# Causal attention scores from three bfloat16 pieces of queries and keys instead of float32 products

## The chip, the cores and the metric

The kernel runs on one core of a Trainium2 chip. A core has five engines that run side by side and meet through semaphores: TensorE (PE in the profile; its weight loads are the rows PEld), VectorE (DVE), ScalarE (ACT), GpSimd (POOL) and SyncE (SP), which issues transfers. TensorE multiplies a stationary matrix, loaded first, with a moving one, and writes to PSUM, which has eight banks of 512 float32 columns. VectorE and ScalarE read PSUM; GpSimd works on SBUF. The metric is the device time of one execution in microseconds. Three runs of the kernel before took 2534.42, 2536.99 and 2536.26 us, median 2536.26.

## The reference

Two layers, each an attention-like part and a feed-forward part, on one sequence of 2048 rows of 128 numbers: a linear recurrence with a gate, a mixture of 8 experts, causal attention with 16 heads of 8 numbers, and a stack of six blocks with windowed attention of 32 rows and a gated feed-forward. The change touches the causal attention alone. Cut to what matters, it computes

```
qkv = x @ W_qkv + b_qkv
q, k, v = jnp.split(qkv, 3, axis=-1)          # then 16 heads of 8 numbers each
scores = jnp.einsum('bhqd,bhkd->bhqk', q, k) * scaling
scores = jnp.where(mask[None, None, :, :], scores, -jnp.inf)
probs = jax.nn.softmax(scores, axis=-1)
out = jnp.einsum('bhqk,bhkd->bhqd', probs, v)
return out.transpose(0, 2, 1, 3).reshape(b, t, c) @ W_o + b_o
```

## The kernel before

`front` runs the recurrence, and a small planner (`Merge`, which pops jobs by due times that the program gives) interleaves the experts, the projections of keys and values and the first of the attention. `stages123` then runs the attention, and `stage4` the six blocks with an order written out by hand. On each engine the instructions run in the order in which the program records them.

The 16 heads stand in `NGRP` = 4 groups of four. A group's keys and queries lie in SBUF with a head's 8 numbers in 32 partitions of their own, so that the products of four heads use four different quarters of TensorE's rows. The rest of each 32 partitions is zero but for one: partition 8 holds 1 in the keys and, once it is known, minus the row's maximum in the queries, so that the second product gives score minus maximum.

There are 16 blocks, a group of heads by 512 query rows (`blocks`). For each block two generators make units:

- `maxima(b)` first projects the block's queries (`pq`, and ScalarE writes `qT` with bias and scale). Then, for each 128 query rows and each chunk of up to 512 keys, it multiplies with the queries as the stationary side (`sc1`), adds the causal mask on the last chunk by a bfloat16 product, and VectorE reduces the maximum. `finish` transposes the maxima (`ptm`) and adds them to the queries.
- `attend(b)` takes 128 keys by up to 512 query rows, with the keys as the stationary side (`sc2`). ScalarE takes the exponential into `ex`, GpSimd zeroes the masked part of the diagonal tiles (`affine_select`), and `weigh` multiplies with the values into `av` in pieces of up to 256 columns.

`attention` pairs the units. A mixed unit has two halves, each with two heads of a maxima unit and the other two heads of an attend unit: four products, the exponentials, a due piece of `av`, the maxima. `catch_up` issues maxima units alone where the maxima are not far enough ahead, and at the end of a block attend units stand alone. All these products rotate through seven PSUM banks (`psum_s`); `av` has the eighth.

`keys` projects a group's keys for 512 rows and ScalarE writes `kT` with the bias. The buffer of `kT` also holds states of the recurrence before that (`ys`, `yt` through `kf`). `_layouts` prepares the weights' arrangement and the bias columns on the host.

Of the kernel before, what the change touches and what calls it, by code (L numbers as in the profile page):

```python
# [93 lines left out]
class Kernel:  # L94
# [102 lines left out]
    def load3(self, w):  # L197
        nc, a = self.nc, self.a
        wqk = w.tile([P, 2, NGRP, P], F32, name="wqk")
        nc.sync.dma_start(wqk, a["wqk1"])  # L200
        bqk = w.tile([P, 2, NGRP], F32, name="bqk")
        nc.sync.dma_start(bqk, a["bqk1"])
        wv = w.tile([P, P], F32, name="wv1")
        nc.sync.dma_start(wv, a["L1_attn_W_qkv"][:, 2 * P : 3 * P])
        wo = w.tile([P, P], F32, name="wo1")
        nc.sync.dma_start(wo, a["L1_attn_W_o"])
        bo = w.tile([P, 1], F32, name="bo1")
        nc.sync.dma_start(bo, a["bo1"])
        self.w3 = wqk, bqk, wv, wo, bo
# [243 lines left out]
    def keys_values(self, pool, psum, x, g, hT3, kT, va):  # L453
        wqk, bqk, wv, wo, bo = self.w3
        hg = hT3[:, g * GW : (g + 1) * GW]
        yield from self.norm_transposed(pool, psum, x, g, hg)
        pv = psum.tile([P, G, P], F32, name="pv", tag="b")
        self.add_row(pv, 1)
        for j in range(G):
            self.pe.matmul(  # L460
                pv[:, j, :], lhsT=hg[:, j * P : (j + 1) * P], rhs=wv, start=False, stop=j == G - 1
            )
        self.dve.tensor_copy(
            va[:, g * G : (g + 1) * G, :, 0:HD1], pv.rearrange("p j (h d) -> p j h d", d=HD1)
        )
        yield 1.3
        yield from self.keys(psum, g, hT3, kT, [0])

    def keys(self, psum, g, hT3, kT, grps):
        wqk, bqk, wv, wo, bo = self.w3  # L470
        hg = hT3[:, g * GW : (g + 1) * GW]
        for grp in grps:
            pk = psum.tile([P, GW], F32, name="pk", tag="b")
            self.pe.matmul(pk, lhsT=wqk[:, 1, grp, :], rhs=hg, start=True, stop=True)
            self.act.activation(
                kT[:, grp, g * GW : (g + 1) * GW], pk, AF.Identity, bias=bqk[:, 1, grp : grp + 1]
            )
            yield 0.9

    def front(self, ctx, merge, psum, kvpool, x, hT3, kT, va, xsT):  # L480


        nc, tc, gps = self.nc, self.tc, self.gps
        bqk = self.w3[1]
        pool_ = ctx.enter_context(tc.tile_pool(name="s1", bufs=2))
# [18 lines left out]
        half = CL * 2 * NCH  # L504
        kf = kT.rearrange("p n t -> p (n t)")
        ys = kf[:, 0:half].rearrange("p (l c k) -> p l c k", c=2, k=NCH)
# [5 lines left out]
        for g in range(NG):  # L512
# [7 lines left out]
        gps.tensor_scalar_mul(w4[:, 2, :], w4[:, 2, :], vec[:, 3:4])  # L520
        gps.tensor_scalar_mul(bqk[:, 0, :], bqk[:, 0, :], HD1 ** -0.5)
        gps.iota(
            self.iota, pattern=[[1, P]], base=-1024, channel_multiplier=0, allow_small_or_imprecise_dtypes=True
# [7 lines left out]
        self.ssm_carry(pool, pw, rows, zy, u)  # L531

        begin = [(0, 9, 43, 51), (10, 22, 58, 66), (7, 41, 74, 87), (16, 57, 91, 111)]
        def ones():
# [6 lines left out]
        for g, (a, b, c, d) in enumerate(begin):  # L541
            wait.append(merge.add(a, self.ssm_out(pool, psum, x, g, gate, own[g], u)))
            wait.append(merge.add(b, self.experts(pool, psum, x, g)))
            merge.add(c, self.keys_values(kvpool, psum, x, g, hT3, kT, va))
            merge.add(d, self.keys(psum, g, hT3, kT, range(1, NGRP)))
        return wait

    def stages123(self, x, xT):
        nc, tc, a = self.nc, self.tc, self.a
        scale = HD1 ** -0.5  # L550
        with ExitStack() as ctx:
# [13 lines left out]
            hT = keep.tile([P, T], F32, name="hT3")  # L565
            kT = keep.tile([P, NGRP, T], F32, name="kT3")
            va = keep.tile([P, NT, HEADS1, 32], F32, name="va")
# [3 lines left out]
            early.__enter__()  # L571
            wait = self.front(early, merge, banks, kvpool, x, hT, kT, va, xsT)

# [10 lines left out]
            def bank(name):  # L584
                return banks.tile([P, GW], F32, name)
# [4 lines left out]
            ends = [sum(size[: i + 1]) for i in range(len(size))]  # L590
            qs, late = {}, []

# [8 lines left out]


            def maxima(b):
                grp, qc = blocks[b]
                if b % NG == 0:
                    qs[grp] = pool.tile([P, T], F32, name="qT3", tag="qT3")
                q = qs[grp]
                cols = slice(qc * GW, (qc + 1) * GW)
                pq = bank("pq")
                pe.matmul(pq, lhsT=wqk[:, 0, grp, :], rhs=hT[:, cols], start=True, stop=True)  # L610
                act.activation(q[:, cols], pq, AF.Identity, bias=bqk[:, 0, grp : grp + 1], scale=scale)
                nm = nms[b % 2]
                for j in range(G):
                    qt = G * qc + j
# [4 lines left out]
                    def part(pr, ch, qt=qt, mx=mx, chunks=chunks, j=j):  # L619
                        c, wd = chunks[ch]  # L620
                        n = len(chunks)
                        scs = []
                        for h in (2 * pr, 2 * pr + 1):
                            r = slice(32 * h, 32 * h + 32)
                            sc = bank("sc1")
                            pe.matmul(
                                sc[:, :wd], lhsT=q[r, qt * P : (qt + 1) * P], rhs=kT[r, grp, c : c + wd],
                                start=True, stop=ch < n - 1,
                            )
                            scs.append((h, sc))  # L630

                        def rest():
# [4 lines left out]
                            if pr and ch == n - 1:  # L637
                                dve.tensor_reduce(
                                    nm[:, j, :].rearrange("p (h s) -> p h s", s=32)[:, :, HD1],
                                    mx[:, :, 0:n], axis=AX.X, op=ALU.max, negate=True,  # L640
                                )

                        return rest

                    for ch, (_, wd) in enumerate(chunks):
                        yield wd, part, ch

                def finish():
                    pt = bank("ptm")
                    for j in range(G):  # L650
                        pe.transpose(pt[:, j * P : (j + 1) * P], nm[:, j, :], self.ident)
                    dve.tensor_tensor(q[:, cols], q[:, cols], pt, ALU.add)

                yield 0, finish, None


# [3 lines left out]
            def attend(b):  # L660
# [15 lines left out]
                for kt in range(last + 1):  # L676
# [3 lines left out]
                    def part(pr, kt=kt, lo=lo):  # L680
                        nonlocal ex
                        if ex is None:
                            ex = pp.tile([P, 4, GW], F32, name="ex3")
                        for jj in range(2):
                            h = 2 * pr + jj
                            r = slice(32 * h, 32 * h + 32)
                            sc = bank("sc2")
                            pe.matmul(
                                sc[:, lo:], lhsT=kT[r, grp, kt * P : (kt + 1) * P],
                                rhs=q[r, qc * GW + lo : (qc + 1) * GW], start=True, stop=True,  # L690
                            )
                            act.activation(ex[:, h, lo:], sc[:, lo:], AF.Exp)

# [132 lines left out]
            def catch_up(b, c):  # L826
                nonlocal ahead
                while ahead is not None and done - ahead[1] < wanted(b, c) - GW:
                    for rest in [step_m(ahead, pr) for pr in range(2)]:
                        rest()  # L830
# [8 lines left out]
            def attention():  # L839
                nonlocal ahead, halves  # L840
                b_now, c_now = -1, 0
                for b, wd, part, whole in ats:
# [5 lines left out]
                    if ahead is not None and done - ahead[1] < wanted(b, c_now):  # L848
                        for half in range(2):
                            rest = step_m(ahead, half)  # L850
                            part(1 - half)
                            weigh_due()
# [6 lines left out]
                    else:  # L859
                        for half in range(2):  # L860
                            part(1 - half)
                        weigh_due()
# [542 lines left out]
def _layouts(x):  # L1405
# [16 lines left out]
    wqk = np.zeros((P, 2, NGRP, 4, 32), f)  # L1422
    wqk[..., :HD1] = x["L1_attn_W_qkv"][:, : 2 * P].reshape(P, 2, NGRP, 4, HD1)
    got["wqk1"] = wqk.reshape(P, 2, NGRP, P)
    bqk = np.zeros((2, NGRP, 4, 32), f)
    bqk[..., :HD1] = x["L1_attn_b_qkv"][: 2 * P].reshape(2, NGRP, 4, HD1)
    bqk[1, ..., HD1] = 1.0
    got["bqk1"] = bqk.reshape(2, NGRP, P).transpose(2, 0, 1)
    got["bv1"] = x["L1_attn_b_qkv"][2 * P :].reshape(1, P)
# [30 lines left out]
```

## Time and profile before

| | before |
|---|---|
| median of three runs | 2536.26 us |
| the profiled execution's own time | 2534.71 us |
| its span | 2533.0 us |
| mean granted TensorE clock | 0.975 |
| TensorE busy | 2423.0 us (96%) |
| VectorE busy | 1844.1 us (73%) |
| ScalarE busy | 1728.4 us (68%) |
| GpSimd busy | 1471.4 us (58%) |

The profiler records start and end of each instruction of one execution. A row of a group names engine and operation, the tiles written and read (`sc<-kT,qT`), the shapes and the count. Since every instruction passes through one helper, all have line L66, and one goes by tiles. A matmul's end is modelled, so the distance from one start to the next says more than its length. In the trace both kinds of products write a tile `sc`: `sc<-kT,qT` with keys moving is that of the maxima, `sc<-qT,kT` that of the exponentials. In a window's row, the columns are the length, busy time and instructions of PE, PEld, DVE, ACT and POOL, the granted clock, the share of the DMA engines and GB/s.

### The profile page before, as it was taken

The page shows a single profiled execution, that of the slowest core. Times are in us where ns is not written, and L with a number is a line of the kernel's source. Part 1 is how long each engine was busy: PE and PEld are TensorE (multiplying, and loading weights), DVE is VectorE, ACT ScalarE, POOL GpSimd, SP SyncE. Part 2 cuts the span into 40 slices and gives each one's busy share as a digit, 9 for nine tenths or more (in the row PEclk, how much of TensorE's full clock was granted, in tenths as well). Part 3 has the DMA queues.
Part 4 walks back from the last instruction along what each step waited for, and adds up shares of the span by engine and source line. Part 5 has one row for each costly group of instructions (what it writes and reads, how often), then busy time and mean ns, then how long its engine had stood idle before and what let it go on. Part 6 is the DMA issues. An engine that isn't in the chain of part 4 may idle for free.

```text
span 2533.0 us, 87720 instructions
## 1 busy us (share of the span) xinstructions
PE 2423.0 (96%) x38312; PEld 1441.2 (57%) x38312; DVE 1844.1 (73%) x2519; ACT 1728.4 (68%) x3233; POOL 1471.4 (58%) x1007
## 2 busy tenths in 40 slices
PE   5689999999999799999999999999999999999997
PEld 3663333333334466666666666666666666666665
DVE  7667765467653488887888778877888778878874
ACT  3323455634556377887888878887888788888884
POOL 3210000100001699888888878887888888888880
PEclk8889999989999899999999999999999999999999
DMA  2000000000000422233223322242223322222221
GB/s 79 1 1 1 1 1 1 1 1 2 1 1 1 103 70 71 68 90 77 70 70 78 93 62 70 66 101 66 72 67 91 76 70 70 67 60 64 65 68 38
DMA packets 100157, 130.13 MB, mean 51 GB/s; under 512 B 26553, under 2 KB 47681, under 8 KB 99777
## 3 DMA queue, kind: packets, MB, share of 16 engines
q1 hardware_dynamic: 99196, 124.07, 19.8%
q8 instruction: 304, 4.98, 0.9%
q14 instruction: 77, 0.62, 0.1%
q10 hardware_dynamic: 580, 0.46, 0.1%
HBM read 23.50 MB, written 1.05 MB: 10 GB/s over the span
## 4 chain that ended last, share of the span: by engine, by line
PE 90%; DVE 4%; ACT 3%; POOL 1%; issue 1%; DMA 0%; ACTq 0%; DVEq 0%; POOLq 0%
PE sc L66 21%; PE ps L66 14%; PE po L66 9%; PE pt L66 7%; PE pv L66 7%; PE px L66 7%; PE av L66 6%; PE ph L66 5%; PE py L66 4%; PE ptp L66 3%; PE prb L66 1%; PE pvar L66 1%; PE pm L66 1%; ACT ex L66 1%; DVE kT L66 1%
## 5 line engine op out<-in xcount | busy, mean ns | idle before, releaser
L66 POOL TENSOR_TENSOR rn<-ss,mhalf 128x32 f32<-128x32 f32 x96 | 524.2, 5460 | 8.0
L66 ACT ACTIVATE sm<-sm,mx,rn 128x64 f32<-128x64 f32 x1536 | 519.8, 429 | 3.7 <-POOL mx L66 3.0
L66 DVE TENSOR_REDUCE mx<-sc 128x1 f32<-128x512 f32 (+3 forms) x640 | 353.5, 604 | 222.3 <-PE sc L66 220.9
L66 ACT ACTIVATE ex<-sc 128x512 f32<-128x512 f32 (+3 forms) x640 | 306.1, 537 | 281.5 <-PE sc L66 280.4
L66 POOL TENSOR_TENSOR rot_a<-rot_a,rot_b 128x1024 f32<-128x1024 f32 x192 | 449.9, 2361 | 5.7 <-DVE rot_b L66 5.7
L66 PE MATMUL sc<-kT,qT 64*32 64x64 f32 (+2 forms) x13568 | 442.0, 259 | 8.6 <-ACT qT L66 7.8
L66 PE MATMUL ps<-wqkv,s 128*128 128x512 f32 x768 | 395.3, 619 | 2.0 <-DVE s L66 1.6
L66 POOL TENSOR_SCALAR_AFFINE_SELECT ex<-ex 128x512 f32<-128x512 f32 x64 | 40.6, 635 | 576.0 <-ACT ex L66 560.2
L66 PE MATMUL sc<-qT,kT 32*128 32x512 f32 (+3 forms) x1280 | 339.1, 581 | 4.0 <-DVE qT L66 2.1
L66 DVE TENSOR_TENSOR rot_a<-ps,tab 128x1024 f32<-128x1024 f32 x192 | 234.8, 1223 | 127.1 <-ACT sq L66 122.0
L66 PEld LDWEIGHTS sc<-kT,qT 64*32 64x32 f32 (+1 forms) x13568 | 219.5, 113 | 188.6 <-issue 108.7
L66 PEld LDWEIGHTS po<-pT,vw 64*64 64x64 f32 x12288 | 210.5, 135 | 184.9 <-issue 175.6
L66 ACT ACTIVATE sq<-ps 128x1024 f32<-128x1024 f32 x192 | 196.5, 1023 | 134.3 <-PE ps L66 97.1
L66 PE MATMUL po<-pT,vw 64*64 64x32 f32 x12288 | 242.1, 222 | 4.6 <-ACT pT L66 4.2
L66 DVE TENSOR_TENSOR rot_b<-ps,tab 128x1024 f32<-128x1024 f32 x192 | 232.9, 1213 | 0.0
L66 DVE TENSOR_REDUCE ss<-sq 128x16 f32<-128x1024 f32 x192 | 224.6, 1211 | 1.1
L66 PE MATMUL pt<-ident,rot_a 128*128 128x128 f32 x1536 | 211.4, 281 | 11.6 <-POOL rot_a L66 11.5
L66 PEld LDWEIGHTS pt<-ident,rot_a 128*128 128x128 f32 x1536 | 170.8, 142 | 46.4 <-issue 23.7
L66 PE MATMUL pv<-wqkv,s 128*128 128x512 f32 x384 | 190.6, 619 | 0.0
L66 PE MATMUL px<-oT,wo 64*128 64x128 f32 x3072 | 185.8, 276 | 0.8 <-DVE ot L66 0.8
L66 POOL TENSOR_TENSOR rot_a<-rot_a,rn 128x1024 f32<-128x1024 f32 x96 | 182.6, 1902 | 0.1
L66 PEld LDWEIGHTS px<-oT,wo 64*128 64x128 f32 x3072 | 176.6, 189 | 9.0 <-issue 4.5
(212 smaller groups left out, 3481.8 us busy)
## 6 DMA issues: line engine op xcount, KB each, us to landing
vw<-vt SPq DMA_DIRECT2D x1524, 64.0 KB, 2.0
wqkv<-in_L_ffn_Wqkv SPq DMA_DIRECT2D x18, 512.0 KB, 5.5
wo<-in_L_ffn_Wo SPq DMA_DIRECT2D x24, 256.0 KB, 6.0
w<-in_L_ffn_W SPq DMA_DIRECT2D x6, 341.0 KB, 3.6
x<-in_L_attn_hidden_states SPq DMA_DIRECT2D x4, 256.0 KB
out<-ot SPq DMA_DIRECT2D x4, 256.0 KB, 2.3
rot<-in_rot SPq DMA_DIRECT2D x1, 960.0 KB
w<-in_L_ffn_W SPq DMA_DIRECT2D x12, 64.0 KB, 4.9
```

Of the source, the lines that this page charges most:

```text
L66: return self._tc.keep_in_program_order(call(*args, **kw))
```

## The change

Queries and keys are no longer float32 but three bfloat16 pieces: the value rounded, the remainder rounded, and the remainder of that. A head's 32 partitions hold the three pieces of a key in partitions 0 to 23 (8 each), and ones in 24 to 26. The queries have three copies, `q[:, 0]`, `q[:, 1]` and `q[:, 2]`, and copy i repeats piece i in partitions 0 to 7, 8 to 15 and 16 to 23. A product of copy i with the keys so adds piece i times all three key pieces, and three products accumulated in PSUM make all nine pairs. The maximum, too, is split in three pieces, in partitions 24 to 26 of copy 0.

- `keys` has, after ScalarE's instruction, one of VectorE that forms the remainder (`krest`) and two of GpSimd that form the second piece and write `kT`. The bias table `bqk` has two more rows: the bias where ScalarE writes, and zeros and ones that choose partitions.
- `project` replaces the projection in `maxima`: ScalarE writes copy 0, VectorE the remainder (`qrest`), GpSimd copies 1 and 2. It is called for the next block after the first unit of a block (for the first block at its start), and the scale is folded into `wqk`.
- A unit's `part` returns its products as functions, and `products` issues them in turn: the first product of all heads, then the second, then the third. In a mixed half that is two heads of either kind, elsewhere four heads of one kind. Each product is now a weight load and a matmul of their own.
- The maxima of a block collect in `m`, and `pieces_of` splits them with six GpSimd instructions into `nm`.
- `kT` and the queries of head groups 0 and 2 share the buffer that `kf` had; those of groups 1 and 3 have one of their own.

```diff
     def keys(self, split, psum, g, hT3, kT, grps):
...
+            one, two = (split.tile([P, GW], BF16, name=f"k{i}") for i in range(2))
+            rest = split.tile([P, GW], F32, name="krest")
             self.act.activation(
-                kT[:, grp, g * GW : (g + 1) * GW], pk, AF.Identity, bias=bqk[:, 1, grp : grp + 1]
+                one, pk, AF.Identity, bias=bqk[:, 2, grp : grp + 1], scale=bqk[:, 3, 0:1]
             )
+            self.dve.scalar_tensor_tensor(rest, pk, bqk[:, 1, grp : grp + 1], one, ALU.add, ALU.subtract)
+            self.gps.tensor_scalar_mul(two, rest, bqk[:, 3, 1:2])
+            self.gps.tensor_tensor(kT[:, grp, g * GW : (g + 1) * GW], rest, two, ALU.subtract)
...
+        gps.tensor_scalar_mul(wqk[:, 0], wqk[:, 0], HD1 ** -0.5)
...
+            def project(b):
+                grp, qc = blocks[b]
+                q, cols = qs[grp], slice(qc * GW, (qc + 1) * GW)
+                pq = bank("pq")
+                pe.matmul(pq, lhsT=wqk[:, 0, grp, :], rhs=hT[:, cols], start=True, stop=True)
+                rest = pool.tile([P, GW], F32, name="qrest")
+                act.activation(q[:, 0, cols], pq, AF.Identity, bias=bqk[:, 0, grp : grp + 1])
+                dve.scalar_tensor_tensor(
+                    rest, pq, bqk[:, 0, grp : grp + 1], q[:, 0, cols], ALU.add, ALU.subtract
+                )
+                gps.tensor_copy(q[:, 1, cols], rest)
+                gps.tensor_tensor(q[:, 2, cols], rest, q[:, 1, cols], ALU.subtract)
+
+            def products(heads):
+                for i in range(3):
+                    for product in heads:
+                        product(i)
...
-                            pe.matmul(
-                                sc[:, :wd], lhsT=q[r, qt * P : (qt + 1) * P], rhs=kT[r, grp, c : c + wd],
-                                start=True, stop=ch < n - 1,
-                            )
+                            def product(i, r=slice(32 * h, 32 * h + 32), sc=sc):
+                                pe.matmul(
+                                    sc[:, :wd], lhsT=q[r, i, qt * P : (qt + 1) * P], rhs=kT[r, grp, c : c + wd],
+                                    start=i == 0, stop=i == 2 and ch < n - 1,
+                                )
...
                     for ch, (_, wd) in enumerate(chunks):
                         yield wd, part, ch
+                        if j == 0 and ch == 0 and b + 1 < len(blocks):
+                            project(b + 1)
...
+            def pieces_of(m, nm):
+                out = nm.rearrange("p j (h s) -> p j h s", s=32)
+                for i in range(2):
+                    piece = pool.tile([P, G, 4], BF16, name="m_piece")
+                    gps.tensor_copy(piece, m)
+                    gps.tensor_copy(out[:, :, :, 3 * HD1 + i], piece)
+                    left = m if i == 0 else out[:, :, :, 3 * HD1 + 2]
+                    gps.tensor_tensor(left, m, piece, ALU.subtract)
...
                         for half in range(2):
-                            rest = step_m(ahead, half)
-                            part(1 - half)
+                            m_heads, rest = step_m(ahead, half)
+                            heads, exps = part(1 - half)
+                            products(m_heads + heads)
+                            exps()
                             weigh_due()
```

## The prediction

> **What bounds the kernel now.** I read the page first: the TensorE row of part 2 and the chain in part 4.
>
> ```profile
> PE 2423.0 (96%) x38312; PEld 1441.2 (57%) x38312; DVE 1844.1 (73%) x2519; ACT 1728.4 (68%) x3233; POOL 1471.4 (58%) x1007
> ...
> PE   5689999999999799999999999999999999999997
> ...
> PE 90%; DVE 4%; ACT 3%; POOL 1%; issue 1%; DMA 0%; ACTq 0%; DVEq 0%; POOLq 0%
> ```
>
> TensorE sets the time nearly everywhere. The change lies in the causal attention, from the first `sc` group at 183 us to about 823 us, so next I cut the span there.
>
> ```profile
> 0.00:183.00 183.00, 127.09 (x761) 98.27 (x761) 131.10 (x369) 58.00 (x150) 47.88 (x123) 0.88 0.09 28
> 183.00:823.00 640.00, 623.44 (x5407) 241.28 (x5407) 378.32 (x748) 329.92 (x681) 42.95 (x66) 0.97 0.01 1
> ```
>
> The columns after the length are busy PE, PEld, DVE, ACT and POOL, then granted clock. In the attention PE is busy 97%, VectorE 59%, GpSimd 7%. Shorter products therefore show, until VectorE's maxima limit. Third, one stretch in order of time (start, length):
>
> ```profile
> 269.37 1.56 PE L66 MATMUL sc<-kT,qT 32*128 32x512 f32 x10
> ...
> 270.53 4.87 DVE L66 TENSOR_REDUCE mx<-sc 128x1 f32<-128x512 f32 x8 [0.41 <-PE sc L66]
> 270.76 0.59 PE L66 MATMUL sc<-kT,qT 32*128 32x512 f32 x2
> ...
> 275.29 0.70 PE L66 MATMUL sc<-kT,qT 32*128 32x512 f32 x2
> ...
> 275.30 0.70 PE L66 MATMUL sc<-qT,kT 32*128 32x512 f32 x2
> ...
> 275.82 0.59 PE L66 MATMUL sc<-kT,qT 32*128 32x512 f32 x2
> 275.83 0.59 PE L66 MATMUL sc<-qT,kT 32*128 32x512 f32 x2
> ```
>
> A float32 product is two records (passes). Four heads start within 20 ns, at 275.29, and their second passes start together 0.53 later; the first of these contains about 0.10 of weight load. At 269.37 ten records fill 1.56: two groups of four and two more, with passes 0.43 apart once rolling: 269.91, 270.34 and, in the line shown, 270.76. Eight maxima back to back take 4.87, 0.60 each. Fourth, what a full-array pass and bfloat16 cost:
>
> ```profile
> 1132.09 1.88 PE L66 MATMUL ps<-wqkv,s 128*128 128x512 f32 x4
> ```
>
> ```profile
> 116.41 0.40 PE L66 MATMUL pi<-ident,which 128*128 128x128 bf16 x4 [1.49 <-DVE which L66]
> ```
>
> ```profile
> 88.36 0.39 PE L66 MATMUL pl<-row,one 3*128 3x512 bf16 x1
> 88.67 0.38 PE L66 MATMUL pl<-wg,hT 128*128 128x128 f32 x1
> ```
>
> A lone float32 pass is (1.88-0.59)/3 = 0.43, the same as four side by side. A bfloat16 pass over 128 columns is (0.40-0.22)/3 = 0.06, load included; over 512 it is 0.31 less one hand-over of about 0.10, so 0.21. Last, the waits of the attention:
>
> ```profile
> PEld sc L66 <- DVE mx L66: 54.0, 128, 2.3
> ...
> PEld sc L66 <- ACT qT L66: 15.2, 10, 1.6
> ...
> PEld sc L66 <- ACT ex L66: 11.1, 38, 0.7
> PE sc L66 <- ACT qT L66: 7.0, 9, 0.8
> ```
>
> Seven PSUM banks rotate and a group takes four; its fourth product waits for an earlier maximum.
>
> **The change, part by part.** *Products.* A group of four 512-column products lasts 1.07 from its start to the next thing on PE: two passes of 0.43, load 0.10, hand-over 0.11. It becomes three rounds of bfloat16. Nothing before runs four of those together, so the ends are 0.21 a round (the `pl` row) and 0.43 (the float32 pass): groups of 0.84 and 1.50. I take 0.22, since the float32 rows show four side by side costing nothing: group 0.87. Counted in the program's order there are 314 groups; with the wider partner counted, they make 299 of 512 columns. By kind:
> - 27 groups of four maxima products, with the two mixed groups that follow: 5.92 from 269.37 to 275.29. The eight maxima (4.8) end last, so I take 4.9: 27 x -1.0 = -27.
> - 82 other mixed groups without a mask: 1.64 and 1.88 in turn, 1.76 on average. After: 0.87 and the `av` piece's 0.57, 1.44, above VectorE's 2 x 0.60. I take -0.32 for 65 of them and -0.2 for 17 with a narrow half: -24.
> - 103 mixed groups with a mask: 1.86, of which `av` and mask are 0.79. -0.20 each: -20.
> - 39 of four exponentials: ScalarE needs 4 x 0.49 and the step lasts 2.1: -0.1 each, -4. The 8 masked maxima-only groups: -1.
>
> Together -76. If a round is 0.21 it is -85. At 0.43 each of the 299 costs +0.43, +129, of which the waits for banks would take back perhaps 40.
>
> *Query projections moved a block ahead.* Today PE stands about 0.78 between `pq` and the next group, until ScalarE has written `qT`. In the new order that product works for the next block. The cover is a whole block's maxima, some 20 us. 14 x 0.78: -11 (0 to -12). What is late next is the bank: `pq` is now also read by VectorE.
>
> *Query pieces.* 16 VectorE instructions of 128x512 from PSUM (0.75 by the `act` row, 0.99 by `own`), 12 to 16 us, and two GpSimd ones each (`x<-x,ye` took 1.26). GpSimd has 597 us idle here and nobody waits for a block. Behind VectorE's instruction maxima queue; where they end last it counts in full, elsewhere not at all. Take half, +6 (0 to 16).
>
> *Key pieces.* 16 such VectorE instructions too, and on GpSimd a tensor_scalar (0.94 at 128x256, so about 1.9) and a tensor_tensor, 3.1 us a job. The remainder tile has two buffers, so the third key job of a run can hold VectorE until GpSimd is through the first; behind it stand the experts' masks and behind GpSimd's pieces the norms' powers (1.0 each). Most falls before 260 us, where VectorE is 70% busy. Take +8, between 0 (all beside PE's work) and 25 (the 12 to 16 and a 2 us stall in four runs).
>
> *Maxima in pieces.* Six small GpSimd instructions a block (0.22, the `mx<-mx,rn` row), 1.3 us, behind an affine_select of 0.64, before the transposes `ptm`. PE reaches these one unit, 2.9 us, later; the reserve is under 1 us. The transposes stand ahead of everything else on PE. Take 16 x 0.4 = +6 (0 to 20).
>
> *The first block* has no cover: its pieces pass VectorE and GpSimd before PE may load them, +3 (0 to 4). The wider `bqk` load and the extra scaling of `wqk` on GpSimd run in the first 100 us beside work that nobody waits for: 0; uncovered, below 2.
>
> Sum: -76 - 11 + 6 + 8 + 6 + 3 = -64. The profiled execution took 2534.7 (span 2533.0 and 1.7 around it), 1.5 under the median of 2536.3. So 2470.7 against it and **2472** against the median.
>
> **A rule against it.** The rows above show no loss from four float32 passes side by side. The Trainium skill, "TensorE: Matmul & The Clock Gate", Part 3, measured only 3.07 times for four 32-row tiles of 512 columns. By the rows, a round is 0.22; by the rule, estimated, 0.29, the group 1.08, and the products would gain nothing: about 2535 to 2545.
>
> **Rivals.** *The bfloat16 rounds don't run side by side at full speed* (the other side). Place: every group. Price 299 x (3t + 0.21 - 1.07); with the other terms it turns the sum at about t = 0.29. For it: four writers into PSUM at twice the rate of any row here. Against it: four cost the same as one in float32. At t = 0.43, 2534.7 + 129 - 40 + 12 = 2636.
>
> *PE's queue becomes the bound.* A mixed half has 28 instructions instead of 8, since loads stand apart. The `pi` row issues a load and a product every 0.06, which gives 0.84 a half, below 1.44. At 0.08 an instruction a half is 2.24, +0.4 on some 240 halves: 2620. It decides from 0.063.
>
> *The banks keep the pace.* With all rounds of a group behind its fourth product's wait, a half would be 0.87 + 0.09 + 0.68 + 0.07 = 1.71 instead of 1.76 (VectorE's start 0.09 after the end, the maximum, the wake). For it: 54.0 us of such waits. Against it: the fourth head waits for the first head's maximum, and that head can end two rounds after the wait, not three. Price: the 119 unmasked 512-column halves outside and inside the 27 runs gain only 0.05, -6, the masked ones still -20, with -11 and +23: 2521.
>
> **How the numbers follow.** Forecast (gain 30 to 110) 0.70; the banks 0.10, nearly all of it still faster; within 0.2% (5 us, about what a measurement tells from no change) 0.04; slower rounds 0.11, the queue 0.03, the added pieces outweighing all 0.02. Faster 0.80, same 0.04, slower 0.16. The low end is the -85 with -12 and costs near nothing, and VectorE's stretches at their floor: 2425. At the top the slower cases above 2545 hold about 1 in 10. The forecast's own range is 2425 to 2505.
>
> **What would show it.** Right: `sc` records in bfloat16 with rounds 0.22 apart, plain halves near 1.44, eight maxima still 4.87, PE's wait for `qT` gone, the attention near 580 us, and the time after 823 us unchanged. Wrong: rounds of 0.3 or more; `issue` ahead of `sc`; PE waiting for GpSimd before `ptm`; the stretch before 183 us longer by more than 10.

## The result, and the profile after

Four runs of the changed kernel took 2492.18 to 2495.29 us, median 2493.35; the kernel before took 2536.01 beside it. The ratio is 0.9833, 95% interval 0.9816 to 0.985: 1.7% faster, by about 43 us. The profiled execution took 2495.29, with a span of 2493.6 and a mean granted clock of 0.965.

The first look is the page of the changed kernel: TensorE's row of part 1 and of part 2, and the chain of part 4.

```profile
PE 2338.7 (94%) x39592; PEld 1402.0 (56%) x39592; DVE 1866.7 (75%) x2551; ACT 1724.7 (69%) x3233; POOL 1561.9 (63%) x1168
...
PE   5678999989998799999999999999999999999997
...
PE 82%; DVE 8%; POOL 3%; ACT 3%; issue 3%; DMA 0%; POOLq 0%; ACTq 0%; DVEq 0%
```

TensorE is busy 84 us less, but the span fell by only 39. Its share of the chain fell from 90 to 82%, and VectorE's rose from 4 to 8%, GpSimd's from 1 to 3%: where products became shorter, other engines now end the wait. The second look cuts the span at the first and the last exponential (columns as in the windows of before).

```profile
0.00:206.00 206.00, 139.08 (x793) 106.54 (x793) 141.04 (x381) 59.50 (x151) 78.38 (x152) 0.82 0.08 25
206.00:782.00 576.00, 526.49 (x6666) 193.57 (x6665) 390.70 (x768) 325.66 (x683) 103.05 (x198) 0.96 0.01 2
```

Two things of opposite sign stand side by side. The attention, from the first exponential to the last, takes 576.1 where it took 638.8 (823.7 - 184.9): 62.7 less. The first exponential comes at 206.0 instead of 184.9: 21.1 more. What follows the attention lasts 1711.5 against 1709.3.

The third look is one mixed half of the changed kernel in order of time (start, length).

```profile
400.24 0.39 PE L66 MATMUL sc<-kT,qT 32*128 32x512 bf16 x2
400.24 0.39 PE L66 MATMUL sc<-qT,kT 32*128 32x512 bf16 x2
400.46 0.38 PE L66 MATMUL sc<-kT,qT 32*128 32x512 bf16 x2
...
400.68 0.38 PE L66 MATMUL sc<-kT,qT 32*128 32x512 bf16 x2
...
400.99 0.64 PE L66 MATMUL av<-ex,va 128*32 128x256 f32 x8
```

Two heads of either kind start together, and the rounds are 0.22 apart. From the first product to the `av` piece a group lasts 0.75, less than the forecast 0.87 and the 1.07 of before.

Fourth, one run of four maxima products and the two mixed halves after it, of the changed kernel.

```profile
304.07 1.07 PE L66 MATMUL sc<-kT 32*128 32x512 bf16 x15
304.93 5.07 DVE L66 TENSOR_REDUCE mx<-sc 128x1 f32<-128x512 f32 x8 [0.23 <-PE sc L66]
305.67 0.80 PE L66 MATMUL sc<-kT 32*128 32x512 bf16 x9 [0.53 <-DVE mx L66]
...
306.97 0.86 PE L66 MATMUL sc<-kT 32*128 32x512 bf16 x3
308.06 0.80 PE L66 MATMUL sc<-kT 32*128 32x512 bf16 x9 [0.23 <-DVE mx L66]
...
309.37 0.89 PE L66 MATMUL sc<-kT 32*128 32x384 bf16 x12
```

The 15 records at 304.07 are the group's twelve and the first three of the first half, which start at 304.73. The second half's first three heads start at 306.97; its fourth head waits until 308.06 for a bank that an earlier maximum holds. With the next half at 309.37, the three steps last 0.66 + 2.25 + 2.39 = 5.30. In the stretch shown of before, the two halves start at 270.34 and 272.90:

```profile
270.34 0.19 PEld L66 LDWEIGHTS sc<-kT,qT 32*128 32x128 f32 x2 [0.19 <-issue]
...
272.90 0.70 PE L66 MATMUL sc<-kT,qT 32*128 32x512 f32 x2
```

There the same three steps were 0.96 + 2.56 + 2.39. The 2.39 is the same in both, four maxima of 0.60.

### The profile page after: what moved, and what is told of

Read it like the earlier page. It is cut to its first block, busy times and chain, and to the rows that moved or that the text cites. A ratio compares the mean times of both kernels' runs of the same rounds, so it can differ in the third digit from the quotient of the medians.

```text
span 2493.6 us, 90478 instructions
## 1 busy us (share of the span) xinstructions
PE 2338.7 (94%) x39592; PEld 1402.0 (56%) x39592; DVE 1866.7 (75%) x2551; ACT 1724.7 (69%) x3233; POOL 1561.9 (63%) x1168
## 4 chain that ended last, share of the span: by engine, by line
PE 82%; DVE 8%; POOL 3%; ACT 3%; issue 3%; DMA 0%; POOLq 0%; ACTq 0%; DVEq 0%
PE ps L66 14%; PE sc L66 14%; PE po L66 9%; PE pt L66 8%; PE pv L66 7%; PE px L66 7%; PE ph L66 5%; PE av L66 5%; DVE mx L66 4%; PE py L66 4%; PE ptp L66 3%; ACT ex L66 1%; PE pvar L66 1%; PE prb L66 1%; PE pm L66 1%
## 5 line engine op out<-in xcount | busy, mean ns | idle before, releaser
L66 PE MATMUL sc<-kT,qT 64*32 64x64 f32 (+2 forms) x13248 | 274.6, 234 | 0.5 <-ACT kT L66 0.5
L66 PE MATMUL sc<-kT 32*128 32x512 bf16 (+3 forms) x1920 | 192.4, 359 | 23.9 <-DVE mx L66 19.5
L66 PE MATMUL av<-ex,va 128*32 128x256 f32 (+1 forms) x2432 | 179.7, 376 | 4.9 <-POOL ex L66 4.1
L66 PEld LDWEIGHTS ps<-wqkv,s 128*128 128x128 f32 x768 | 127.2, 194 | 94.8 <-issue 52.8
```

The lines of the kernel that those rows point to most:

```text
L66: return self._tc.keep_in_program_order(call(*args, **kw))
```

## The experiments

The kernel before stood at 2535 to 2541 in the series below, so kernels of different series are compared by their ratios to it; a ratio times 2536 gives the time in the series of the result. The changed kernel has 0.9833. Milestones come from the traces: `own` is the first VectorE instruction of the experts' masks after 138 us, "first ex" the first exponential.

| kernel | median us | ratio (95%) | `own` | first ex | last ex |
|---|---|---|---|---|---|
| before | 2536.01 | 1 | 138.88 | 184.9 | 823.7 |
| changed | 2493.35 | 0.9833 (0.9816-0.9850) | 146.22 | 206.0 | 782.1 |
| keys_one | 2472.18 | 0.9735 (0.9706-0.9764) | 139.14 | 188.3 | 757.9 |
| rest_4bufs | 2490.20 | 0.9811 (0.9792-0.9829) | 145.96 | 201.2 | 771.3 |
| keys_no_gps | 2489.93 | 0.9798 (0.9784-0.9813) | 146.23 | 202.3 | 778.2 |
| keys_off_dve | 2495.86 | 0.9823 (0.9801-0.9844) | 138.81 | 201.3 | 780.7 |
| second_on_act | 2493.67 | 0.9817 (0.9797-0.9837) | 150.07 | 207.6 | 783.3 |
| half_max_after | 2435.69 | 0.9593 (0.9569-0.9616) | 144.96 | 201.6 | 723.8 |
| half_max_before | 2501.00 | 0.9847 (0.9827-0.9866) | 143.03 | 185.8 | 784.3 |
| max_direct | 2491.99 | 0.9806 (0.9774-0.9838) | 147.85 | 206.3 | 776.9 |
| pq_ahead_f32 | 2529.86 | 0.9972 (0.9956-0.9988) | 143.41 | 187.4 | 817.4 |
| head_by_head | 2496.39 | 0.9832 (0.9787-0.9876) | 146.24 | 205.9 | 781.9 |
| all_off_dve | 2515.60 | 0.9914 (0.9891-0.9938) | 138.80 | 203.1 | 798.2 |
| max_one_round | 2495.42 | 0.9831 (0.9806-0.9857) | 146.39 | 202.5 | 778.7 |

### Where the 21 us ahead of the attention come from

**keys_one** takes the key pieces away: keys of one piece, written by ScalarE alone.

```diff
-            one, two = (split.tile([P, GW], BF16, name=f"k{i}") for i in range(2))
-            rest = split.tile([P, GW], F32, name="krest")
             self.act.activation(
-                one, pk, AF.Identity, bias=bqk[:, 2, grp : grp + 1], scale=bqk[:, 3, 0:1]
+                kT[:, grp, g * GW : (g + 1) * GW], pk, AF.Identity, bias=bqk[:, 1, grp : grp + 1]
             )
-            self.dve.scalar_tensor_tensor(rest, pk, bqk[:, 1, grp : grp + 1], one, ALU.add, ALU.subtract)
-            self.gps.tensor_scalar_mul(two, rest, bqk[:, 3, 1:2])
-            self.gps.tensor_tensor(kT[:, grp, g * GW : (g + 1) * GW], rest, two, ALU.subtract)
```

> The changed kernel with keys of one bfloat16 piece: ScalarE writes kT directly, and the 16 VectorE and 32 GpSimd instructions of the other two key pieces are left out, so the scores have only the first piece of the keys. Theory A (the key pieces cost what the traces put between them, the first exponential 21 us later and four stalls of VectorE for the remainder's buffer): the first exponential is back near 188 us and the time falls by 16 to 22, to 2472 to 2477. Theory B (the key pieces cost the 8 us of the prediction, and the rest of the delay is the first block's query pieces or run to run): it falls by 5 to 10, to 2484 to 2488.

The first exponential is back at 188.3, and the ratio falls by 0.0098, about 25 us. So the key pieces cost some 18 us ahead of the attention, and more in all than their forecast of 8. What is left ahead of the attention, 3.4, is near the +3 that the first block was given; in pq_ahead_f32, below, which has no pieces and only projects the second block's queries earlier, the same milestone moved by 2.5.

Where they cost it, VectorE's instructions in order of time show. First the changed kernel:

```profile
139.08 1.42 DVE L66 SCALAR_TENSOR_TENSOR krest<-pk,bqk,k 128x512 f32<-128x512 f32 x2 [0.45 <-ACT k L66]
140.41 0.73 DVE L66 TENSOR_SCALAR hot<-pi,e_col 8x512 f32<-8x512 f32 x1
142.78 0.75 DVE L66 SCALAR_TENSOR_TENSOR krest<-pk,bqk,k 128x512 f32<-128x512 f32 x1 [1.63 <-POOL kT L66]
145.56 0.75 DVE L66 SCALAR_TENSOR_TENSOR krest<-pk,bqk,k 128x512 f32<-128x512 f32 x1 [2.03 <-POOL kT L66]
146.22 2.47 DVE L66 SCALAR_TENSOR_TENSOR own<-pi,hT 128x512 f32<-128x512 f32 x4
```

and the kernel before:

```profile
138.21 0.74 DVE L66 TENSOR_SCALAR hot<-pi,e_col 8x512 f32<-8x512 f32 x1 [0.62 <-PE pi L66]
138.88 2.46 DVE L66 SCALAR_TENSOR_TENSOR own<-pi,hT 128x512 f32<-128x512 f32 x4
```

VectorE takes its instructions in order. `own`, the experts' masks, needs nothing of the keys, but it stands behind four remainders and comes 7.3 later; TensorE's expert products (`py`) wait for it. Four remainders are 3.0 us of work; the rest is waiting inside the queue. The brackets name GpSimd's `kT`, that is, the two remainder buffers.

`own` also moves by itself: in half_max_before and pq_ahead_f32, whose keys are those of before, it comes at 143.0 and 143.4, because all that stands ahead is some 4 us later in these executions. Counted from a kernel's first key product (`pk`), it comes after 2.8 us before and in keys_one, after 3.0 in these two, and after 10.2 in the changed kernel; the first exponential comes after 48.8, 52.0, 45.8 and 47.0, and after 70.0 in the changed kernel. So the delay belongs to the key pieces and not to a single execution.

**rest_4bufs** gives the remainder four buffers. Room comes from writing the first two pieces into the key tile itself.

```diff
-            one, two = (split.tile([P, GW], BF16, name=f"k{i}") for i in range(2))
-            rest = split.tile([P, GW], F32, name="krest")
+            one = two = kT[:, grp, g * GW : (g + 1) * GW]
+            rest = split.tile([P, GW], F32, name="krest", bufs=4)
```

> The changed kernel with four buffers for the key remainder instead of two (room is made by writing the first two pieces into the key tile itself). Theory S: the stall of VectorE behind the remainder buffer, 7.3 us of waits in four stretches, is what lies on the path; the first product comes 6 to 8 us earlier and the time falls to 2485 to 2488. Theory L: the pieces' own length (GpSimd 2.7 a job, 16 jobs, VectorE 0.75) and the products put off with them cost the 21 us; then the buffer moves less than 3 us.

The first exponential comes 4.8 earlier, but `own` hardly moves, and the ratio's interval overlaps that of the changed kernel. So the buffers are at most those 5 us of it: the fourth remainder now waits for ScalarE's `kT`, as this line of rest_4bufs shows.

```profile
145.29 0.75 DVE L66 SCALAR_TENSOR_TENSOR krest<-pk,bqk,kT 128x512 f32<-128x512 f32 x1 [3.84 <-ACT kT L66]
```

**keys_no_gps** takes GpSimd out of the keys instead; VectorE writes the remainder straight into the key tile, and the third piece is left out.

```diff
-            rest = split.tile([P, GW], F32, name="krest")
...
-            self.dve.scalar_tensor_tensor(rest, pk, bqk[:, 1, grp : grp + 1], one, ALU.add, ALU.subtract)
-            self.gps.tensor_scalar_mul(two, rest, bqk[:, 3, 1:2])
-            self.gps.tensor_tensor(kT[:, grp, g * GW : (g + 1) * GW], rest, two, ALU.subtract)
+            self.dve.scalar_tensor_tensor(
+                kT[:, grp, g * GW : (g + 1) * GW], pk, bqk[:, 1, grp : grp + 1], one, ALU.add, ALU.subtract
+            )
```

> The changed kernel with the key pieces formed by ScalarE and VectorE alone: VectorE writes the remainder straight into the key tile, and GpSimd's two instructions a job are gone (leaves out the third piece of the keys: the second stands in its place). With VectorE's and GpSimd's part both gone the first exponential had come 18 us earlier (188.3 against 206.0). Theory D: VectorE's 0.75 a job, in the middle of the chain of the experts' masks, is the cost; the first exponential stays at 201 to 206 and the time at 2485 or more. Theory G: GpSimd's 2.7 a job and VectorE's wait for it are the cost; the first exponential comes at 188 to 193 and the time is 2472 to 2480.

Theory G falls: without any GpSimd work in the keys the first exponential still comes at 202.3. The ratio is 0.0035 lower, about 9 us, with intervals that just do not overlap. VectorE's lines of this kernel show what takes the buffers' place:

```profile
145.56 0.75 DVE L66 SCALAR_TENSOR_TENSOR kT<-pk,bqk,k 128x512 bf16<-128x512 f32 x1 [3.66 <-ACT k L66]
146.23 1.88 DVE L66 SCALAR_TENSOR_TENSOR own<-pi,hT 128x512 f32<-128x512 f32 x3
```

The fourth remainder waits 3.66 for ScalarE, which waits for the key product, and the waits of this stretch (engine, for whom: us in total, times, longest) name that too:

```profile
ACT k L66 <- PE pk L66: 3.9, 1, 3.9
...
PE py L66 <- DVE hot L66: 1.8, 1, 1.8
```

That is a detour through three queues: on TensorE the last key product stands behind the first `py`, which waits for `hot` on VectorE; `hot` stands behind two remainders; and then `own` stands behind the remainder of that last key product. TensorE idles meanwhile, and its granted clock between 136 and 150 us is 0.72 in the changed kernel and 1.00 before (0.84 and 0.83 in half_max_before and pq_ahead_f32). The last key product lasts 1.13 before and 2.08 in the changed kernel, where the granted clock from 142.5 to 144.5 is 0.50; before and after:

```profile
140.10 1.13 PE L66 MATMUL pk<-hT,wqk 128*128 128x512 f32 x2
```

```profile
142.47 2.08 PE L66 MATMUL pk<-hT,wqk 128*128 128x512 f32 x2
```

So a part of the 21 us is not waiting. Ahead of the first exponential TensorE is busy 139.1 us in the changed kernel, and 128.7 to 134.8 in the kernel before, keys_one, half_max_before and pq_ahead_f32, with nearly the same work. By these figures an estimated 4 to 10 of the 21 are products that last longer at a lower clock; that the waiting brought the clock down was not tested.

**keys_off_dve** takes VectorE out: ScalarE writes the first piece, the key in float32 and the second piece, GpSimd subtracts. **second_on_act** leaves the remainder on VectorE and moves only the second piece from GpSimd to ScalarE, one job behind, with four buffers. The first edit goes on from the second:

```diff
+        def finish():
+            out, rest = ready.pop()
+            self.act.activation(out, rest, AF.Copy, scale=bqk[:, 3, 1:2])
+            self.gps.tensor_tensor(out, rest, out, ALU.subtract)
...
             if ready:
                 finish()
             ready.append((out, rest))
-            self.dve.scalar_tensor_tensor(rest, pk, bqk[:, 1, grp : grp + 1], out, ALU.add, ALU.subtract)
+            self.act.activation(rest, pk, AF.Identity, bias=bqk[:, 1, grp : grp + 1])
+            self.gps.tensor_tensor(rest, rest, out, ALU.subtract)
             if grp == grps[-1]:
                 finish()
```

> The changed kernel with nothing of the key pieces on VectorE: ScalarE writes the first piece, the key with its bias in float32 and the second piece (about 0.7 each), GpSimd the two subtractions (1.15 each). By theory D the first exponential comes at 190 to 196 and the time is 2474 to 2484, the better version of the two kernels. By theory G, 2.3 us a job stay on GpSimd instead of 2.7, and the time stays at 2487 to 2494.

> As with four buffers, and the second key piece is written by ScalarE (about 0.7 us beside 0.3 busy share there) instead of by GpSimd's 1.57 us form, one job behind. If GpSimd's 2.7 us a job is the cost (theory L), a job takes 1.15 there, the first product comes 10 to 15 us earlier and the time is 2478 to 2485; if only VectorE's extra 0.75 us a job and the later order cost, no more than with four buffers alone.

second_on_act gains no more than the four buffers alone, as its second branch has it. keys_off_dve misses theory D's 2474 to 2484: its ratio means 2491, inside the 2487 to 2494 of theory G, which keys_no_gps had refuted. Its `own` is on time at 138.81, as theory D has it, yet the first exponential comes at 201.3. The delay has moved to the norms:

```profile
152.90 1.12 DVE L66 TENSOR_SCALAR ln_h<-x,ln_mv,ln_r 128x128 f32<-128x128 f32 x4 [4.88 <-POOL ln_r L66]
```

GpSimd is now occupied by key pieces from 139 to 152 and does the norm's power `ln_r` behind them, and VectorE waits 4.88 for that. So each single relief brings the first exponential 5 us at most (second_on_act none), and keys_one, without all of it, 18. That fits one chain that passes through VectorE and GpSimd in turn, so that key work ahead of it in either queue delays it. What each link costs is not shown: half_max_after, below, also brings the first exponential 4.4 earlier, without touching the keys.

### What sets the pace in the attention

**half_max_after** and **half_max_before** let VectorE read half of a maximum's columns.

```diff
-                                dve.reduce_max(mx[:, h, ch : ch + 1], sc[:, :wd], axis=AX.X)
+                                dve.reduce_max(mx[:, h, ch : ch + 1], sc[:, : wd // 2], axis=AX.X)
```

> The changed kernel, where each maximum reads half of its columns (leaves out half of the keys in the maximum; the products are all there). In the changed kernel 115 plain halves take 1.65 us on average, though PE's own part is about 0.75 + 0.57 = 1.32. Theory V: VectorE's maxima (0.60 each, two a half, and their banks) set the pace of the halves; with 256 columns they take about 0.38, plain halves fall to about 1.40, the 27 triples of groups to PE's own pace, and the time falls by 30 to 60 us, to 2435 to 2465. Theory P: PE's own queue and hand-overs set it (loads, 28 instructions a half); then the time stays within 5 us of 2493.

> The kernel before with the same edit (leaves out half of the keys in the maximum). If PE bounds the attention before, as the busy share of 97% says, shorter maxima free only the ends of the 27 triples, where eight maxima end last: 5 to 25 us, 2511 to 2531. If the maxima already set the pace there, the gain is as large as in the changed kernel, 30 us or more.

The changed kernel gains 2.4% from it (0.9593 / 0.9833 = 0.9756), about 61 us, and the kernel before 1.5%, about 39. Theory V holds in the changed kernel, and the maxima already had a large part in the pace before, where I had expected 5 to 25. In the chain of work that ended last, VectorE's `mx` holds 18.2% of the attention after the change, 1.0% before, and 3.6% in half_max_after. By starts on TensorE, the mean of a step. The first two rows are the 12 runs in which an unmasked group of four maxima products has two unmasked halves of 512 columns behind it and no other maxima group ahead of it; in the other rows steps with other work on TensorE are left out.

| step | before | changed | half_max_before | half_max_after |
|---|---|---|---|---|
| first half after four maxima products | 2.57 | 2.40 | 2.35 | 1.99 |
| second half after them | 2.39 | 2.39 | 1.64 | 1.33 |
| plain halves of 512 columns elsewhere | 1.73 | 1.45 | 1.62 | 1.32 |
| masked halves elsewhere | 1.79 | 1.53 | 1.75 | 1.51 |

With short maxima the changed kernel's plain halves run at TensorE's own pace, 0.75 + 0.57, as these lines of half_max_after show (0.76 from the products to `av`, 0.57 from there to the next half):

```profile
277.00 0.83 PE L66 MATMUL sc<-kT 32*128 32x512 bf16 x12
277.76 0.64 PE L66 MATMUL av<-ex,va 128*32 128x256 f32 x8
278.33 0.83 PE L66 MATMUL sc<-kT 32*128 32x512 bf16 x12
```

Outside the runs the changed kernel is nearer that pace anyway (1.45). Most of the loss lies in the runs. The granted clock in the attention rises with short maxima, too, from 0.958 to 0.974 and before from 0.974 to 0.991; by these shares, as an estimate, at most 11 us of either gain are products at a higher clock.

**pq_ahead_f32** is the kernel before with the projection one block ahead, alone.

```diff
+            def project(b):
+                grp, qc = blocks[b]
...
             def maxima(b):
...
+                if b == 0:
+                    project(b)
...
                         yield wd, part, ch
+                        if j == 0 and ch == 0 and b + 1 < len(blocks):
+                            project(b + 1)
```

> The kernel before with one part of the change alone: the query projection is issued one block ahead, all in float32. Theory A (PE's 0.78 us of waiting behind each of 14 projections goes): 2536 - 11 = 2525, between 2523 and 2528. Theory B (the wait only moves to the banks, since the projection's bank is then held while mixed groups want it): 2533 to 2537.

It gains 0.28%, 7 us (3 to 11). That is less than the 11 that I took, and the interval just reaches it.

**max_direct** takes the pieces of the maxima away: VectorE writes `nm` itself.

```diff
-                                dve.tensor_reduce(m[:, j, :], mx[:, :, 0:n], axis=AX.X, op=ALU.max, negate=True)
-                                if j == G - 1:
-                                    pieces_of(m, nm)
+                                dve.tensor_reduce(
+                                    nm[:, j, :].rearrange("p (h s) -> p h s", s=32)[:, :, 3 * HD1],
+                                    mx[:, :, 0:n], axis=AX.X, op=ALU.max, negate=True,
+                                )
```

> The changed kernel with the maximum written by VectorE straight into nm, as before the change: the six GpSimd instructions of a block that split it are left out, and the queries carry only the first bfloat16 piece of the maximum. Theory A (the transposes of the maxima wait for GpSimd on PE, 11 to 16 us in the waits of the changed kernel): the time falls by 10 to 16, to 2477 to 2483. Theory B (PE would at that place wait for VectorE or a bank anyway, and the price is the 6 us of the prediction or less): it falls by 0 to 6.

Its ratio is 0.0027 lower, 7 us, but the intervals overlap; in the traces the last exponential comes 5.2 earlier. The forecast +6 fits, and so would zero.

**head_by_head** gives each head its three products in succession.

```diff
-                for i in range(3):
-                    for product in heads:
+                for product in heads:
+                    for i in range(3):
                         product(i)
```

> The changed kernel with each head's three products issued one after the other, then the next head's. Theory A (TensorE starts matmuls in the order of the program, so a head's first product starts with the third of the head before it): a group of four 512-column heads lasts 9 x 0.216 + 0.09 = 2.0 instead of 0.75, on some 299 such groups +1.2 us each, of which little is hidden: 2750 to 2870. Theory B (the quarters of the array have queues of their own, as two passes of a float32 product seem to show): rounds still start together, 2490 to 2500.

The time does not change, and the trace of the same half shows why (head_by_head, in order of time):

```profile
400.22 0.40 PE L66 MATMUL sc<-kT,qT 32*128 32x512 bf16 x2
400.24 0.40 PE L66 MATMUL sc<-qT,kT 32*128 32x512 bf16 x2
400.44 0.38 PE L66 MATMUL sc<-kT,qT 32*128 32x512 bf16 x2
```

The last two heads' first products start at 400.24, before the first head's second at 400.44, though they are issued after it.

**all_off_dve** goes on from keys_off_dve and takes the query remainders off VectorE too.

```diff
-                dve.scalar_tensor_tensor(
-                    rest, pq, bqk[:, 0, grp : grp + 1], q[:, 0, cols], ALU.add, ALU.subtract
-                )
+                act.activation(rest, pq, AF.Identity, bias=bqk[:, 0, grp : grp + 1])
+                gps.tensor_tensor(rest, rest, q[:, 0, cols], ALU.subtract)
```

> As the one before, and the remainder of the queries too is formed by ScalarE (0.7 a block more) and GpSimd (1.15 more) instead of by VectorE (0.75). Theory V, which says that VectorE's maxima set the pace of the attention, expects 5 to 12 us less than the one before, 16 times 0.75 at most. If VectorE's spare time takes the query remainders, no difference within 3 us; if GpSimd's longer chain is late for the next block, slower.

It is 0.9% slower than keys_off_dve, about 23 us: the forecast from theory V was wrong, and only its last clause names the side. In the trace, waits of the `av` weight loads for `ex`, which GpSimd masks, rise from 7.2 to 17.5 between 260 and 740 us, and the 24 steps of four exponentials alone take 2.10 each instead of 1.66, together 10 us. Which of ScalarE's and GpSimd's added instructions costs which part was not separated.

**max_one_round** leaves out two of the three rounds of the maxima's products, so that a maximum comes from the first query piece only; the maxima's pieces are gone as in max_direct and the remainder has four buffers.

```diff
                             def product(i, r=slice(32 * h, 32 * h + 32), sc=sc):
+                                if i:
+                                    return
                                 pe.matmul(
                                     sc[:, :wd], lhsT=q[r, i, qt * P : (qt + 1) * P], rhs=kT[r, grp, c : c + wd],
-                                    start=i == 0, stop=i == 2 and ch < n - 1,
+                                    start=True, stop=ch < n - 1,
                                 )
```

> The changed kernel with four buffers for the key remainder, the maxima written without pieces, and one round of the maxima's products instead of three (only the first piece of the query is used for the maximum, and the maximum is rounded to bfloat16 as it is added; a shift that is the same above and below the division cancels). PE has a third of the rounds less in every half, which would be 0.44 us in the groups of four maxima, while VectorE reads as many columns as before. Theory V, that VectorE's maxima and their banks set the pace of the attention: 5 to 25 us below the 2490 of four buffers alone, most of it from banks that come free earlier, 2465 to 2485. Theory P, PE's own products set it: each mixed half and each group of maxima falls by 0.1 to 0.4, 40 us or more, below 2450.

Both theories missed: less work, and 2495.42. Windows of 5 us of this kernel show it (the seventh figure, after POOL's, is the granted clock):

```profile
275.00:280.00 5.00, 3.56 (x44) 1.59 (x42) 4.04 (x8) 2.71 (x6) 2.23 (x3) 0.88 0.02 3
280.00:285.00 5.00, 5.00 (x32) 1.12 (x28) 1.85 (x8) 2.17 (x4) 0.00 (x0) 0.50 0.00 0
285.00:290.00 5.00, 4.74 (x32) 1.08 (x30) 4.89 (x11) 1.10 (x3) 0.00 (x0) 0.50 0.00 0
```

After two pauses of TensorE (0.74 and 0.65 us, between 276.6 and 278.8) the clock is halved. There a plain half takes 2.41 instead of 1.33, with rounds 0.43 apart. Of the `av` matmuls over 256 columns, 376 last over 0.6 us in this kernel and 76 in the changed one, eight to a half: some 37 more halves at half clock, each about 1.0 longer. By that estimate the lower clock costs about 38 us, more than the 5 to 25 that theory V gave to the smaller work. What keeps the clock down there was not tested.

No variant here that keeps all pieces of the keys and takes the maxima over all keys is clearly faster than the changed kernel.

## Why the prediction was right, and where its sizes were off

The forecast was 2472 and the time is 2493: the sign and the mechanism hold, the gain is 43 instead of 64. The sum puts 75 of gain into the attention (-76, -11, +6, +6) and a loss of 11 at most ahead of it (+8, +3); the traces show 62.7 and 21.1. The attention "near 580" that was named as a sign does not follow from that sum, which gives 638.8 - 75, about 564; that 576.1 lies near it is chance.

| step | forecast us | measured |
|---|---|---|
| four products side by side | group 0.87, rounds 0.22 | 0.75, rounds 0.22 |
| 82 plain halves | -24 | about -22 (1.73 to 1.45 where both sides have 512 columns) |
| masked halves | -0.20 each | -0.26 each (1.79 to 1.53) |
| steps of four exponentials | -4 | -6 (24 steps, 1.92 to 1.68) |
| 27 runs of four maxima products and two halves | -27 | about -13 (0.30 + 0.17 + 0.00 each) |
| projection a block ahead | -11 | -7 (-3 to -11), alone |
| maxima in pieces | +6 | +7, not told from 0 |
| key pieces | +8 | +18 ahead of the attention, about 25 in all (16 to 33 by the intervals) |
| first block | +3 | 3.4 in keys_one, not told from the 2.5 of pq_ahead_f32 |
| query pieces | +6 | not measured alone, see below |

**The products.** The rounds are what the float32 rows had suggested, and the plain and masked halves came out about as summed. The rival with slower rounds is refuted by the 0.22, and so are rounds of 0.29, the estimate drawn from the Trainium skill's 3.07 times ("TensorE: Matmul & The Clock Gate", Part 3): four tiles of 32 rows and 512 columns run here at 0.22, with no loss that these lines show. The queue rival is refuted by plain halves of 1.39 and 1.51 in turn.

**The runs of four maxima products.** The failed step is "the eight maxima (4.8) end last, so I take 4.9". The eight maxima do take 5.07, but TensorE's three steps do not shrink to them: the second half's fourth head starts when it has the bank of a maximum, and that is four maxima, 2.39, after the first half's fourth head (308.06 and 305.67), before and after the change alike. The rival with the banks had this mechanism and priced it in all 119 unmasked halves, outside and inside the runs; it holds inside them, and the plain halves outside did gain. The half-column kernels confirm it, since 2.39 becomes 1.64 and 1.33 there. It is 14 us of the miss.

**The key pieces.** The sentence "the third key job of a run can hold VectorE until GpSimd is through the first; behind it stand the experts' masks" named the place. The size was wrong: +8 takes most of it to fall beside PE's work, and only the bound of 25 has a stall, of 2 us in four runs. The lines show 7.3 us for one run of four jobs, and the stall does not come from the buffers alone, because without GpSimd the wait for the key product takes their place. I had counted what the instructions last and one wait, and not that VectorE's queue, by holding the masks, holds TensorE's products ahead of the very key product that VectorE waits for. The bound of 25 was nearer, though not for its reason alone. It is 10 to 17 us of the miss.

**The query pieces** were sized by VectorE's queue, with "nobody waits for a block" for GpSimd. The rows show who waits: GpSimd's mask of `ex` (`affine_select`) stands behind a block's two instructions, and the profile puts a wait of ScalarE's next exponentials down to them. In the changed kernel:

```profile
330.90 1.16 POOL L66 TENSOR_TENSOR qT<-qrest,qT 128x512 bf16<-128x512 f32 x1
332.01 0.63 POOL L66 TENSOR_SCALAR_AFFINE_SELECT ex<-ex 128x512 f32<-128x512 f32 x1
332.10 2.07 ACT L66 ACTIVATE ex<-sc 128x512 f32<-128x512 f32 x4 [0.75 <-POOL qT L66]
```

Between 185 and 825 us the weight loads of `av` wait for masked `ex` 3.5 us in 7 places before and 10.7 in 17 in the changed kernel (11.0 in max_direct, so the pieces of the maxima are not the reason). What this costs was not measured alone.

The runs, the key pieces and the projection are 28 to 35 us of loss against a miss of 21. The masked halves and the exponentials gained some 8 more than taken, which brings it to 20 to 27; the query pieces stay open. Without these 8 the three losses alone would have put the time at 2500 to 2507, at the end of the range, so that it stayed inside was in part luck.

**The projection** gained 4 less than taken, with an interval that reaches the forecast. The milestones after the attention are unchanged, as said. The wait of `ptm` for GpSimd did appear, as the maxima's pieces were priced: between 200 and 760 us TensorE waited 11.4 for it in 11 places, of which max_direct gave back 5 to 7. The sign that was named for a wrong forecast, a stretch before the first exponential longer by more than 10, came true at 21.

## What to carry to other kernels

When a product gets shorter, price each step of the repeating pattern by the resource that releases it, and ask of every bank which read gives it back: 2.39 us of four maxima stayed 2.39 us while a group of products went from 1.07 to 0.75. An instruction put into an in-order queue costs what stands behind it while it waits, and where its input comes from an engine that waits for something behind it, the wait feeds itself: 3.0 us of remainders delayed the masks by 7.3. Moving such work to another engine helped little here, where the chain seems to pass through that queue too.

## What the runs showed of the hardware that I had not expected

- Products in different quarters of TensorE's rows start out of the order of issue: issued head by head, the last two heads' first products start 0.20 before the first head's second (400.24 against 400.44), and four heads still keep rounds of 0.22.
- A kernel with fewer products ran a large part of the attention at half the clock (0.50 from 280 to 290 us, with TensorE shown busy for 9.7 of these 10 us), and by the estimate above lost the gain by it. The Trainium skill, "TensorE: Matmul & The Clock Gate", section "A second HAM failure mode: psum-queue depth-cycling", describes a clock that falls back when TensorE idles briefly between groups while banks rotate. The rows agree with a fall to one half, and show it lasting through windows in which TensorE is shown busy throughout; that short gaps cause it here is not shown.
- The changed kernel pays some of this too: granted clock 0.72 from 136 to 150 us and 0.96 in its attention, where the kernel before had 1.00 and 0.97; the last key product of a run took 2.08 instead of 1.13.
